# Cross-attention, 32 blocks on one core: the energy of a tile kept in one pair of PSUM banks

## The chip, the cores and the metric

The kernel runs on one core of a Trainium2 chip. Its time is the device time of one execution, in microseconds; lower is better. The median of three runs of the kernel before is 2110.47 us (2110.41 to 2111.45). One execution was profiled.

## The reference

For each of 32 blocks b there is an x and a y of 256 channels by 1024 columns, with weights shared by all blocks. In the reference's words, cut to the computation:

```python
x_q = einsum('oc,bcn->bno', w_qk, y)
x_k = einsum('oc,bcn->bon', w_qk, x)
x_v = einsum('oc,bcn->bon', w_v, x) + b_v
energy = einsum('bnc,bcm->bnm', x_q, x_k)                 # 1024 x 1024 a block
attention = softmax(energy, axis=-1)
attention = attention / (1e-07 + attention.sum(axis=1, keepdims=True))
x_r = einsum('bcn,bnm->bcm', x_v, attention)
x_r = relu(einsum('oc,bcn->bon', w_t, x - x_r) + b_t)
return x + x_r
```

All of it is float32. The kernel folds the weights: G = w_qk^T w_qk once, then energy = y^T (G x); and U = (w_t w_v) x plus a bias, so that the output needs one product U times attention and one w_t x.

## The kernel before, in words

**Stages of a block.** (1) *Energy*: eight tiles of 128 rows by 1024 columns (class `Energy`, L411 to L464). (2) *G x of the next block* (class `Keys`, `pg` in the profile), and *U of the next block* (class `Values`, `pu`). (3) *Column sums*: `columns` and `inverse` turn the sums over rows, kept in `acc`, into a row of reciprocals `rc`. (4) *Attention* (class `Attention`, `po`): VectorE multiplies the exponentials by both reciprocals (`normal`), forms sums of quarters (`mix`, tile `et`), and TensorE multiplies.

**Seven products.** G x, U and the attention product are each written as a product of 2x2 quarters with seven quarter products (class `Seven`, methods p1 to p7): products 1, 6, 7 and 4 add up in the accumulator `one`, 5 and 3 in `two`, 2 in `three`. Between them ScalarE keeps copies (`p1s`, `p5s`, `w`) because the next product is added onto the same bank; `p6` must wait for `p1s`, `p3` for `p5s`, and `p7` for `w`. VectorE's `c11`, `c12`, `c22` and ScalarE's `c21` combine them.

**The energy of a tile.** y and G x are each split into three forms (high, low and a mixture) in a reduced float32 type, and the energy comes from three products of equal forms. For each half of 512 columns, `products` issues 2 + 2 + 2 matmuls: forms 0 and 1 into one bank, form 2 into another. `gather` has ScalarE copy the first bank, scaled by -(1+2^-12), to SBUF (tile `es`), and VectorE add the second bank to it with one custom instruction that writes the sum to `e` in SBUF and leaves the running minimum of each row in `nm`. When both halves are there, `exp` (ScalarE) makes the exponentials in place in `e` with the row sum `rs`, and `share` (VectorE) takes the reciprocal `ri` of `rs` and adds `e` times `ri` into `acc`. The loop staggers them: with the products of tile n go `exp` of n-1 and `share` of n-2.

**PSUM.** There are eight banks of 512 float32 columns; `bank(name)` takes the next free one of a rotating pool of eight.

**Order.** `InOrder` (L62 to L76) chains every instruction of TensorE, VectorE, ScalarE and GpSimd behind the one written before it, so each of these engines works in the order of the program text, and almost every row of the profile has the line of this helper, L73; the tiles tell the rows apart. SyncE issues the loads and stores. GpSimd issues the accumulating DMAs (`accumulate`) that form sums and splits in memory, and does U's bias and sums in `factors`. The text around the change, at the end of the energy of a block that has a next one (L728 to L750), is: `g.p1`, `g.p5`, `exp` of tile 7, `share` of tile 6, `g.p2`, `g.c11`, `share` of tile 7, `g.p6`, `columns`, `g.p3`, `g.c12`, `g.p7`, `g.c22`, then `un.p1`, `un.p5`, `un.p2`, `un.p6` and `inverse`. The last block has no next one: there the end of the attention of the block before it (`before.xpart`, `before.epart`) follows the energy.

**Start.** Before the loop the kernel loads the weights, makes G, the transposed weights (`turned_weights`, bank `pt`), their product (`value_weights`, `pw`), and the bias of U (`value_bias`, `pb`, with `bvs` written by VectorE), with the first G x and U among them.

Of the kernel before, what the change touches and what calls it, by code (L numbers as in the profile page):

```python
# [9 lines left out]
F32 = mybir.dt.float32  # L10
F32R = mybir.dt.float32r
AF = mybir.ActivationFunctionType
ALU = mybir.AluOpType
AX = mybir.AxisListType
# [3 lines left out]
def kernel(  # L18
# [23 lines left out]
    B, C, N = x.shape  # L42
    P = 128
    KC = C // P
    NT = N // P
    MB = 512
    MH = N // MB
# [5 lines left out]
    BIG = 3.0e38  # L53
    UP = 4096.0
    UNDER = 1.0 - 2.0**-13
    OVER = 1.0 + 2.0**-12

    const = ctx.enter_context(tc.tile_pool(name="const", bufs=1))
    xp = ctx.enter_context(tc.tile_pool(name="xp", bufs=2))
    ps_m = ctx.enter_context(tc.tile_pool(name="ps_m", bufs=8, space=bass.MemoryType.PSUM))  # L60

    class InOrder:  # L62

# [13 lines left out]

    pe, dve, act, pool = (InOrder(g) for g in (nc.tensor, nc.vector, nc.scalar, nc.gpsimd))

    def bank(name):  # L80
        return ps_m.tile([P, MB], F32, tag="m", name=name)

    loaded = {}

    def load(b, pieces=1):
        to = xp.tile([P, KC, N], F32, tag="x", name=f"x_{b}")
        from_ = x[b].rearrange("(k p) n -> p k n", p=P)
        W = KC // pieces
        for j in range(pieces):
            nc.sync.dma_start(to[:, ts(j, W)], from_[:, ts(j, W)])  # L90
        loaded[b] = to
# [43 lines left out]
    behind = const.tile([P, 1], F32, name="behind")  # L135
    parts = const.tile([P, NB, NG + 1], F32, name="parts")
    dve.memset(parts[:, :, NG], EPS)
    idle = bank("idle")
    for _ in range(5):
        pe.matmul(idle[:, :P], few, few, start=True, stop=True)  # L140
    make_identity(nc, ident)
# [19 lines left out]
        return w, (a11, a12, s4, a22, s1, s2, s3)  # L161


    pg = [bank(f"pg_{i}") for i in range(KC)]
    for i in range(KC):
        for k in range(KC):
            pe.matmul(
# [1 line left out]
            )  # L169
    _, g_left = lefts("g", pg, UP)  # L170

    def turned_weights():

        pt = [bank(f"pt_{i}") for i in range(KC)]
        for i in range(KC):
            for k in range(KC):
                pe.transpose(pt[i][:, ts(k, P)], wt[:, k, ts(i, P)], ident)
        return lefts("wtT", pt)

    def value_weights(wtT):  # L180

        pw = [bank(f"pw_{i}") for i in range(KC)]
        for i in range(KC):
            for k in range(KC):
                pe.matmul(
                    pw[i][:, :C], wv[:, k, ts(i, P)], wtT[:, k, :], start=(k == 0), stop=(k == KC - 1)
                )
        return lefts("wvtT", pw, -1.0)[1]

    def value_bias(wtT):  # L190

        pb = bank("pb")
        for k in range(KC):
            dve.tensor_scalar(bvs[:, k], few, bv[:, k], None, ALU.add)
        for k in range(KC):
            pe.matmul(pb[:, :C], bvs[:, k], wtT[:, k, :], start=(k == 0), stop=(k == KC - 1))
        act.mul(bu.rearrange("p k c -> p (k c)"), pb[:, :C], -1.0)
        act.mul(nbt[:, :, 0], bt[:, :, 0], -1.0)
# [7 lines left out]
    def temp(tag, name):  # L206
        return cp.tile([P, MB], F32, tag=tag, name=name)
# [82 lines left out]
    class Seven:  # L290
# [3 lines left out]
        def __init__(self, name, b):  # L294
            self.name = name
            self.b = b

        def bank(self, j):
            return bank(f"p{self.name}{j}_{self.b}")

        def kept(self, p, tag):
            s = temp(tag, f"{self.name}{tag}_{self.b}")
# [107 lines left out]
    class Energy:  # L410
# [3 lines left out]
        def __init__(self, b, n, yf, gf):  # L414
            self.b, self.n = b, n
            self.yf, self.gf = yf, gf
            self.low = BIG

        def products(self, h):
            self.sums = [bank(f"pe{j}_{self.b}_{self.n}_{h}") for j in range(2)]  # L420
            for j in range(3):
                for k in range(KC):
                    pe.matmul(
                        self.sums[j // 2],
                        self.yf[:, j, k, ts(self.n, P)],
                        self.gf[:, j, k, ts(h, MB)],
                        start=(k == 0 and j != 1),
                        stop=(k == KC - 1 and j != 0),
                    )

        def gather(self, h):


            s = temp(("p1s", "p5s")[h], f"es_{self.b}_{self.n}_{h}")
            act.mul(s, self.sums[0], -OVER)
            nm = sp.tile([P, 1], F32, tag=f"nm{h}", name=f"nm_{self.b}_{self.n}_{h}")
            dve.tensor_tensor_reduce(
                out=e[:, self.n, ts(h, MB)],
                in0=self.sums[1],
                in1=s,  # L440
                scale=1.0,
                scalar=self.low,
                op0=ALU.add,
                op1=ALU.min,
                accum_out=nm,
            )
            self.low = nm

        def exp(self):
            self.rs = sp.tile([P, 1], F32, tag="rs", name=f"rs_{self.b}_{self.n}")  # L450
            row = e[:, self.n, :]
            act.activation(row, row, AF.Exp, bias=self.low, scale=-1.0, accum_out=self.rs)

        def share(self):

# [213 lines left out]
    g.split.high(0)  # L669
    g.split.high(1)  # L670
    u_left = value_weights(wtT)
    for i in range(KC):
        g.split.low(i)
    for i in range(KC):
# [9 lines left out]
    u.p6()  # L684
    u.p3()
    u.p7()
    value_bias(wtT)
    u.c11()
    u.c12()
    u.c22()  # L690
# [2 lines left out]
    for b in range(B):  # L693
        more = b + 1 < B
        rows = []

        for n in range(NT):
            now = Energy(b, n, q.to, g.split.to)
            rows.append(now)
            now.products(0)  # L700
            if n == 0:
                e = ep.tile([P, NT, N], F32, tag="e", name=f"e_{b}")
                acc = one.tile([P, N], F32, tag="acc", name=f"acc_{b}")
            now.gather(0)
            now.products(1)
            now.gather(1)
            if n == 0:
                if b == 0:
                    u.p4()
                    u.c21()  # L710
                    xsteps[1]()
                    xsteps[2]()
                elif more:
                    load(b + 1)
                if b == 0:
                    ur, usteps = u.factors()
                    for step in usteps:
                        step()
                if more and b > 0:
                    xn, xsteps = summed(b + 1)  # L720
            if n > 0:
                rows[n - 1].exp()
            if n > 1:
                rows[n - 2].share()
            if more and b > 0 and n in (2, 4, 6):
                xsteps[n // 2 - 1]()

        if more:  # L728
            q = Queries(b + 1)
            for i in range(KC):  # L730
                q.load(i, nc.sync.dma_start)
            g = Keys(b + 1, xn)
            g.p1()
            g.p5()
            rows[-1].exp()
            rows[-2].share()
            g.p2()
            g.c11()
            rows[-1].share()
            g.p6()  # L740
            columns(b)
            g.p3()
            g.c12()
            g.p7()
            g.c22()
            un = Values(b + 1, xn)
            un.p1()
            un.p5()
            un.p2()
            un.p6()  # L750
        else:
            before.xpart(before.one, 7, True)
            rows[-1].exp()
            rows[-2].share()
            before.epart(before.one, 7)
            ur, usteps = u.factors()
            now = Attention(b, xr, ur)
            now.begin()
            rows[-1].share()
            columns(b)  # L760
            for step in usteps:
                step()
            before.p7s = temp("w", "p7s")
            act.copy(before.p7s, before.one)
        rc = inverse(b)
        if more:
            q.parts(0)
            q.lower(0)
            un.p3()
            g.p4()  # L770
            g.c21()
            un.p7()
            q.parts(1)
            q.lower(1)
            q.mixed(0)
            g.split.parts(0)
            q.mixed(1)
            g.split.lower(0)

            def between():  # L780
                g.split.parts(1)
                g.split.lower(1)
                g.split.mixed(0)
                g.split.mixed(1)

            now = Attention(b, xr, ur)
            now.begin()
            now.run(un, between=between)
            pool.tensor_copy(behind, now.t4[:, HT - 1, :1])
            if b + 2 < B:  # L790
                now.close()
                ur, usteps = un.factors()
                for step in usteps:
                    step()
            else:
                now.epart(now.two, 3, (3,))
                now.c12()
                now.put()
            before = now
            xr, u = xn, un  # L800
        else:
            before.end()
            now.run(None, before)
            now.finish()
# [30 lines left out]
```

## Time and profile before

| | us |
|---|---|
| median of three runs | 2110.47 |
| profiled execution, its own time | 2108.64 |
| its span, first to last instruction | 2106.9 |
| TensorE busy (share of the span) | 2081.3 (99%) |
| VectorE busy | 1815.0 (86%) |
| ScalarE busy | 1171.9 (56%) |
| GpSimd busy | 673.3 (32%) |
| one block, energy start to energy start (1005.65 to 1070.68) | 65.03 |

The granted TensorE clock is at full speed in all of the span. Rows of the timeline give the start of an instruction (or of a run of like ones, with their count), what it took, and in brackets the idle time of the engine before it and what ended that. The start of the next instruction on the same engine is often earlier than the end of the one before, since the engines overlap the end of one with the start of the next; so costs in a queue are read from start to start. "po" is the attention product, "pe" the energy, "pg" G x, "pu" U.

### The profile page before, as it was taken

The page shows a single profiled execution, that of the slowest core. Times are in us where ns is not written, and L with a number is a line of the kernel's source. Part 1 is how long each engine was busy: PE and PEld are TensorE (multiplying, and loading weights), DVE is VectorE, ACT ScalarE, POOL GpSimd, SP SyncE. Part 2 cuts the span into 40 slices and gives each one's busy share as a digit, 9 for nine tenths or more (in the row PEclk, how much of TensorE's full clock was granted, in tenths as well). Part 3 has the DMA queues.
Part 4 walks back from the last instruction along what each step waited for, and adds up shares of the span by engine and source line. Part 5 has one row for each costly group of instructions (what it writes and reads, how often), then busy time and mean ns, then how long its engine had stood idle before and what let it go on. Part 6 is the DMA issues. An engine that isn't in the chain of part 4 may idle for free.

```text
span 2106.9 us, 23473 instructions
## 1 busy us (share of the span) xinstructions
PE 2081.3 (99%) x7586; PEld 1286.3 (61%) x7586; DVE 1815.0 (86%) x3032; ACT 1171.9 (56%) x1794; POOL 673.3 (32%) x574
## 2 busy tenths in 40 slices
PE   8999999999999999999999999999999999999998
PEld 6556665566665666556666556655566655666564
DVE  6898888998888988889888898888998888988898
ACT  5556554566455664556655556554566455664562
POOL 3322333323333133332333322333323333133321
PEclk9999999999999999999999999999999999999999
DMA  4665577665776656766557766577665676656740
GB/s 140 163 127 142 133 175 170 129 145 130 167 173 136 148 132 151 180 159 129 138 134 184 168 123 144 131 175 170 129 147 129 166 179 140 138 131 152 180 95 30
DMA packets 107802, 306.14 MB, mean 145 GB/s; under 512 B 10656, under 2 KB 11424, under 8 KB 107680
## 3 DMA queue, kind: packets, MB, share of 16 engines
q0 software_dynamic: 57040, 170.68, 44.2%
q1 hardware_dynamic: 50496, 133.85, 18.5%
q8 instruction: 60, 0.98, 0.2%
q14 instruction: 62, 0.51, 0.1%
q10 hardware_dynamic: 144, 0.13, 0.0%
HBM read 124.78 MB, written 33.55 MB: 75 GB/s over the span
## 4 chain that ended last, share of the span: by engine, by line
PE 62%; DVE 29%; issue 4%; ACT 1%; DMA 1%; DVEq 0%; POOL 0%; ACTq 0%; POOLq 0%
PE pe L73 31%; PE po L73 29%; DVE e L73 14%; DVE acc L73 4%; DVE et L73 4%; DVE gfr L73 3%; DVE rc L73 2%; DVE sc L73 1%; PE pu L73 1%; DVE parts L73 1%; ACT es L73 1%; DVE ri L73 0%; DMA gf<-gfr 0%; PE pg L73 0%; DMA gf<-gf 0%
## 5 line engine op out<-in xcount | busy, mean ns | idle before, releaser
L73 PE MATMUL pe<-gf,yf 128*128 128x512 f32 x3072 | 715.6, 393 | 0.9 <-DMA gf<-gf 0.9
L73 PEld LDWEIGHTS pe<-gf,yf 128*128 128x128 f32 x3072 | 576.6, 188 | 134.3 <-issue 16.2
L73 ACT ACTIVATE es<-pe 128x512 f32<-128x512 f32 x512 | 304.4, 595 | 172.2 <-PE pe L73 171.9
L73 PE MATMUL po<-et,us 128*128 128x512 f32 x768 | 353.9, 597 | 11.7 <-DVE et L73 11.7
L73 DVE SCALAR_TENSOR_TENSOR e<-e,ri,rc 128x512 f32<-128x512 f32 x512 | 347.4, 745 | 1.1
L73 DVE SCALAR_TENSOR_TENSOR acc<-e,ri,acc 128x1024 f32<-128x1024 f32 x224 | 288.6, 1288 | 8.0
L73 ACT ACTIVATE e<-e,nm 128x1024 f32<-128x1024 f32 x256 | 292.6, 1143 | 0.6 <-DVE nm L73 0.6
L73 PEld LDWEIGHTS po<-et,us 128*128 128x128 f32 x768 | 142.8, 190 | 207.3 <-issue 158.6
L73 DVE CUSTOM_DVE_ANT_0 e<-pe,es,nm 128x512 f32<-128x512 f32 x256 | 192.2, 751 | 76.6 <-ACT es L73 51.5
L73 PE MATMUL po<-e,ut 128*128 128x512 f32 x512 | 225.0, 592 | 1.0 <-DVE e L73 1.0
L73 POOL DMA_DIRECT2D yf<-yfr x62 | 53.1, 857 | 524.0 <-ACT yf L73 508.7
L73 DVE CUSTOM_DVE_ANT_0 e<-pe,es 128x512 f32<-128x512 f32 x256 | 175.5, 686 | 41.5 <-ACT es L73 41.2
L73 ACT ACTIVATE z<-po,bt 128x512 f32<-128x512 f32 x31 | 21.4, 690 | 334.2 <-DMA out_dram<-z 231.8
L73 PEld LDWEIGHTS po<-e,ut 128*128 128x128 f32 x512 | 97.2, 190 | 123.8 <-issue 107.4
L73 DVE TENSOR_TENSOR et<-e 128x1024 f32<-128x1024 f32 x128 | 153.6, 1220 | 4.4
L73 POOL TENSOR_TENSOR ut<-ut,bu 128x1024 f32<-128x1024 f32 x64 | 152.6, 2438 | 0.7 <-ACT ut L73 0.7
L73 POOL DMA_DIRECT2D gf<-gf x62 | 53.1, 856 | 295.5 <-DMA gf<-gfr 255.3
L73 DVE SCALAR_TENSOR_TENSOR z<-z,x 128x512 f32<-128x512 f32 x96 | 128.7, 1341 | 3.3
L73 PE MATMUL po<-e,us 128*128 128x512 f32 x256 | 125.4, 592 | 0.0
L73 ACT ACTIVATE yf<-yf 128x1024 fp32r<-128x1024 f32 x124 | 124.2, 1049 | 2.0
L73 ACT ACTIVATE gf<-gf 128x1024 fp32r<-128x1024 f32 x124 | 124.2, 1049 | 2.0
L73 POOL DMA_DIRECT2D xs<-xs x31 | 37.2, 1201 | 254.6 <-DMA xs<-in_x_dram 245.2
(110 smaller groups left out, 2749.1 us busy)
## 6 DMA issues: line engine op xcount, KB each, us to landing
yfr<-in_ctx_dram SPq DMA_DIRECT2D x64, 512.0 KB, 5.7
out_dram<-z SPq DMA_DIRECT2D x128, 256.0 KB, 3.5
x<-in_x_dram SPq DMA_DIRECT2D x31, 1024.0 KB, 7.5
xs<-in_x_dram SPq DMA_DIRECT2D x62, 512.0 KB, 5.0
yf<-yfr POOLq DMA_DIRECT2D x62, 512.0 KB, 5.1
yf<-yf POOLq DMA_DIRECT2D x62, 512.0 KB, 7.9
gf<-gfr POOLq DMA_DIRECT2D x62, 512.0 KB, 10.3
gf<-gf POOLq DMA_DIRECT2D x62, 512.0 KB, 5.2
```

The costliest lines, as they stand in the source:

```text
L73: self.last = getattr(self.engine, name)(*args, **kwargs)
```

## The change

All eight banks become one tile `banks`, and every user is given its place. A tile's energy has a pair of adjacent banks, one for each half, by its number: pairs 0 to 3 in turn (in the last block pairs 0 to 2). G x sits in banks 0, 1, 2 (those of tiles 4 and 5), U in 3, 4, 5, and the attention product in 6, 7, 1.

Forms 0 and 1 of both halves go to the pair (`first`), ScalarE scales the pair in place in PSUM with one instruction of 1024 columns, and form 2 is then added by TensorE onto the scaled numbers (`second`). VectorE only takes the minimum of 1024 columns from PSUM, and `exp` reads PSUM and writes `e`. Tile 7 is scaled in halves. The loop is staggered by one more: with `first` of tile n go `second` of n-1, `exp` of n-2 and `share` of n-3. At the start, `bvs` is written and `value_bias` done early; U's `p4`, `c21` and `factors` of the first block move from after tile 0 to after tile 1.

```diff
-    ps_m = ctx.enter_context(tc.tile_pool(name="ps_m", bufs=8, space=bass.MemoryType.PSUM))
+    ps_m = ctx.enter_context(tc.tile_pool(name="ps_m", bufs=1, space=bass.MemoryType.PSUM))
+    banks = ps_m.tile([P, 8, MB], F32, name="banks")
-    def bank(name):
-        return ps_m.tile([P, MB], F32, tag="m", name=name)
+    def bank(j):
+        return banks[:, j]
...
     _, g_left = lefts("g", pg, UP)
+    for k in range(KC):
+        dve.tensor_scalar(bvs[:, k], few, bv[:, k], None, ALU.add)
...
     def value_bias(wtT):
-        pb = bank("pb")
-        for k in range(KC):
-            dve.tensor_scalar(bvs[:, k], few, bv[:, k], None, ALU.add)
+        pb = bank(6)
...
+            last = name == "o" and b == B - 1
+            first = name == "u" and b == 0
+            self.places = {
+                "g": (0, 1, 2),
+                "u": (6, 4, 5) if first else (3, 4, 5),
+                "o": (7, 4, 5) if last else (6, 7, 1),
+            }[name]
         def bank(self, j):
-            return bank(f"p{self.name}{j}_{self.b}")
+            return bank(self.places[(1, 5, 2).index(j)])
...
-            self.low = BIG
-        def products(self, h):
-            self.sums = [bank(f"pe{j}_{self.b}_{self.n}_{h}") for j in range(2)]
...
-        def gather(self, h):
...
+            at = 2 * (n % (4 if b + 1 < B else 3))
+            self.pair = banks[:, at : at + 2]
+        def products(self, forms, halves=range(MH)):
+            for h in halves:
+                for j in forms:
+                    for k in range(KC):
+                        pe.matmul(
+                            self.pair[:, h],
+                            self.yf[:, j, k, ts(self.n, P)],
+                            self.gf[:, j, k, ts(h, MB)],
+                            start=(j == 0 and k == 0),
+                            stop=(j == 2 and k == KC - 1),
+                            skip_group_check=True,
+                        )
+        def first(self):
+            if self.n + 1 < NT:
+                self.products((0, 1))
+                act.mul(self.pair, self.pair, -OVER)
+                return
+            for h in range(MH):
+                self.products((0, 1), (h,))
+                act.mul(self.pair[:, h], self.pair[:, h], -OVER)
+        def second(self):
+            self.products((2,))
+            self.low = sp.tile([P, 1], F32, tag="nm", name=f"nm_{self.b}_{self.n}")
+            dve.tensor_reduce(self.low, self.pair.rearrange("p h m -> p (h m)"), AX.X, ALU.min)
         def exp(self):
-            row = e[:, self.n, :]
-            act.activation(row, row, AF.Exp, bias=self.low, scale=-1.0, accum_out=self.rs)
+            act.activation(
+                e[:, self.n, :],
+                self.pair.rearrange("p h m -> p (h m)"),
+                AF.Exp,
+                bias=self.low,
+                scale=-1.0,
+                accum_out=self.rs,
+            )
...
     u_left = value_weights(wtT)
+    value_bias(wtT)
...
     u.p7()
-    value_bias(wtT)
...
             now = Energy(b, n, q.to, g.split.to)
             rows.append(now)
-            now.products(0)
+            now.first()
...
-            now.gather(0)
-            now.products(1)
-            now.gather(1)
-            if n == 0:
-                if b == 0:
-                    u.p4()
-                    u.c21()
-                    xsteps[1]()
-                    xsteps[2]()
-                elif more:
-                    load(b + 1)
-                if b == 0:
-                    ur, usteps = u.factors()
-                    for step in usteps:
-                        step()
-                if more and b > 0:
-                    xn, xsteps = summed(b + 1)
             if n > 0:
-                rows[n - 1].exp()
+                rows[n - 1].second()
+            if b == 0 and n == 1:
+                u.p4()
+                u.c21()
+                xsteps[1]()
+                xsteps[2]()
+                ur, usteps = u.factors()
+                for step in usteps:
+                    step()
+            if more and b > 0 and n == 0:
+                load(b + 1)
+                xn, xsteps = summed(b + 1)
             if n > 1:
-                rows[n - 2].share()
+                rows[n - 2].exp()
+            if n > 2:
+                rows[n - 3].share()
...
             g = Keys(b + 1, xn)
+            rows[-1].second()
+            rows[-2].exp()
+            rows[-3].share()
             g.p1()
-            g.p5()
             rows[-1].exp()
             rows[-2].share()
+            g.p5()
             g.p2()
             g.c11()
             rows[-1].share()
...
         else:
+            rows[-1].second()
+            rows[-2].exp()
+            rows[-3].share()
             before.xpart(before.one, 7, True)
             rows[-1].exp()
             rows[-2].share()
```

More of the change, by code (lines that the diff above doesn't have):

```diff
@@ L137 @@
     dve.memset(parts[:, :, NG], EPS)
-    idle = bank("idle")
+    idle = bank(7)
     for _ in range(5):
@@ L161, in lefts @@
         return w, (a11, a12, s4, a22, s1, s2, s3)
-    pg = [bank(f"pg_{i}") for i in range(KC)]
+    pg = [bank(3 + i) for i in range(KC)]
     for i in range(KC):
@@ L170 @@
     _, g_left = lefts("g", pg, UP)
+    for k in range(KC):
+        dve.tensor_scalar(bvs[:, k], few, bv[:, k], None, ALU.add)
     def turned_weights():
-        pt = [bank(f"pt_{i}") for i in range(KC)]
+        pt = [bank(6 + i) for i in range(KC)]
         for i in range(KC):
@@ L180, in value_weights @@
     def value_weights(wtT):
-        pw = [bank(f"pw_{i}") for i in range(KC)]
+        pw = [bank(4 + i) for i in range(KC)]
         for i in range(KC):
@@ L416, in __init__ @@
             self.yf, self.gf = yf, gf
-            self.low = BIG
-        def products(self, h):
-            self.sums = [bank(f"pe{j}_{self.b}_{self.n}_{h}") for j in range(2)]
[L421 to L429, printed above, removed]
@@ L431, in gather @@
-        def gather(self, h):
[L434 to L447, printed above, removed]
+            at = 2 * (n % (4 if b + 1 < B else 3))
```

## The prediction, made before the changed kernel ran

> **What bounds the kernel now.** I read the page first, then the timeline of one block from the middle (energy from 1006 us) engine by engine, then the start and the last block.
>
> ```profile
> PE 2081.3 (99%) x7586; PEld 1286.3 (61%) x7586; DVE 1815.0 (86%) x3032; ACT 1171.9 (56%) x1794; POOL 673.3 (32%) x574
> ...
> PE 62%; DVE 29%; issue 4%; ACT 1%; DMA 1%; DVEq 0%; POOL 0%; ACTq 0%; POOLq 0%
> ```
>
> TensorE is almost never idle, yet the chain that ended last runs through VectorE for 29%. Both are true because, in each block, a stretch of VectorE work ends just late enough to hold TensorE for a moment. TensorE's timeline:
>
> ```profile
> 1002.62 3.60 PE L73 MATMUL po<-et,ut 128*128 128x512 f32 x8
> 1005.65 22.36 PE L73 MATMUL pe<-gf,yf 128*128 128x512 f32 x96
> 1027.85 1.02 PE L73 MATMUL pg<-x,g 128*128 128x512 f32 x2
> ...
> 1032.14 1.11 PE L73 MATMUL pg<-xs,gs 128*128 128x512 f32 x2
> 1033.08 1.05 PE L73 MATMUL pu<-wvtT,x 128*128 128x128 f32 x8
> ...
> 1048.74 1.88 PE L73 MATMUL po<-et,us 128*128 128x512 f32 x4
> 1050.95 1.98 PE L73 MATMUL po<-et,us 128*128 128x512 f32 x4 [0.33 <-DVE et L73]
> 1052.78 1.02 PE L73 MATMUL po<-xs,wtTs 128*128 128x512 f32 x2
> ```
>
> A pair of float32 matmuls takes 0.86 us from start to start, so one takes 0.429. The eight po from 1002.62 end their slots at 1006.05, and the 96 energy matmuls fill 1006.05 to 1027.85: 0.227 each, 2.72 us a tile, no idle time. p7 of G x (1032.14) needs 0.94 instead of 0.86: 0.08 lost to the copy `w`. The four et matmuls from 1048.74 should end at 1050.45; the next begin at 1050.95 and take 1.83 instead of 1.72: 0.61 lost, waiting for `et`. VectorE, from the last energy matmul to that wait:
>
> ```profile
> 1029.16 0.75 DVE L73 CUSTOM_DVE_ANT_0 e<-pe,es,nm 128x512 f32<-128x512 f32 x1 [0.17 <-DVE nm L73]
> ...
> 1031.23 0.16 DVE L73 RECIPROCAL ri<-rs 128x1 f32<-128x1 f32 x1
> 1031.42 1.28 DVE L73 SCALAR_TENSOR_TENSOR acc<-e,ri,acc 128x1024 f32<-128x1024 f32 x1
> 1032.62 0.68 DVE L73 TENSOR_TENSOR gfr<-pg,gp1s 128x512 f32<-128x512 f32 x1
> 1033.22 0.15 DVE L73 RECIPROCAL ri<-rs 128x1 f32<-128x1 f32 x1
> 1033.41 1.28 DVE L73 SCALAR_TENSOR_TENSOR acc<-e,ri,acc 128x1024 f32<-128x1024 f32 x1
> 1034.73 1.25 DVE L73 TRANSPOSE_TENSOR_REDUCE parts<-acc 128x32 f32<-128x1024 f32 x1
> ...
> 1049.68 1.22 DVE L73 TENSOR_TENSOR et<-e 128x1024 f32<-128x1024 f32 x1
> ```
>
> `columns` begins 6.88 us after the energy's last matmul slot (1034.73 less 1027.85). From there VectorE runs gapless to the `et` that TensorE waits for at 1050.95. So a block lasts as long as this tail of VectorE says: energy end to `columns`, plus a fixed 16.2 us, plus TensorE's rest.
>
> **The energy stage.** Matmuls keep their number and shapes: nothing. VectorE per tile before: two custom instructions and their read-outs, 1.54 us from start to start (1019.48 to 1021.02). After: one minimum of 1024 columns. No row has it; nearest is the 512-column TENSOR_TENSOR from PSUM, 0.68 us long and 0.60 to the next start, and the 1024-column one in SBUF, 1.22 and 1.14. I take 1.14 (1.22 until its result is there). Bounds: 0.76 (the 1024-column `acc<-e,ri`, 764 ns) and 1.37 (two customs of 686). With `share` at 1.39 (1031.23 to 1032.62) VectorE needs 2.53 of the 2.72 a tile instead of 2.93: it no longer lags, but waits for TensorE.
>
> Here the rows and a rule part. The Trainium skill (VectorE: DVE Perf Modes, Rules for kernel authors) calls `tensor_reduce` the slowest VectorE operation on a hot path and advises against it; going by the rule alone, swapping a custom operation for it would cost VectorE time, while by the rows above the stage gets 0.40 us a tile cheaper. No row before shows the reduction itself.
>
> ScalarE per tile before: 0.50 + 0.50 + 1.13. After: the in-place scaling, bounded by two copies (1.00) and by half-length rows (0.60 for 512, 1.05 for 1024: 0.50 + 0.45 = 0.95), and `exp` at 1.13 (1028.15 to 1029.28, from SBUF; a copy of 512 out of PSUM takes 0.59 and the one row out of SBUF 0.72, so I add nothing for PSUM): 2.08 of 2.72. `second` of a tile starts a whole tile period after its `first`, so the scaling has 2.7 us for 1.2: hidden; without that cover it would cost 1.2 a tile. Pairs come free 1.3 us before reuse.
>
> The Trainium skill (ScalarE: Activation LUTs, "What happens when an exp ACTIVATE runs") says that ScalarE writes PSUM faster than SBUF; no row before has such a write. By it the scaling would only get shorter, and the sum stays as it is, for it hides in any case.
>
> **The tail, where it counts.** The stagger is one tile deeper and VectorE now waits for tile 6's `second`, with `share` of tile 4 queued behind. Time from the end of that slot, Z; the energy ends at Z+0.91 (four matmuls). A result is seen 0.26 after its slot (up1s at 1034.23, slot end 1033.97). Queue: minimum 6 at 0.26, share 4 at 1.40, minimum 7 at 2.79, share 5 at 3.93, share 6 at 5.32, `c11` at 6.71 (0.60), share 7 at 7.31, `columns` 1.51 later (1033.22 to 1034.73) at 8.82. That is 7.91 after the energy, against 6.88: the block is 1.03 us longer by VectorE's tail.
>
> **TensorE meets a new wait as well.** `p3` needs `p5s`, which ScalarE now does after `exp` of tile 7, which needs minimum 7: its result at 4.01, `exp` at 4.05, `p5s` at 5.18 to 5.77, and a matmul 0.15 later (in p7's case `gw` ended at 1032.07 and the slot slid to 1032.22): 5.92. TensorE arrives after `second` 7, p1, p5, p2, p6: 0.91 + 4 x 0.857 = 4.34. Wait: 1.58. It absorbs p7's 0.08 and up to 0.61 of the `et` wait, so by this path a block is 0.89 longer. The longer path counts, not the sum: 1.03, with 1.58 at p3 and some 0.14 left at `et`. `p6` finds `p1s` at 3.3, before 3.48. G x's banks are read out by `exp` 4 and 5 before Z+1. ScalarE's splits and the DMAs behind them (yf, gf) follow U's copies and so shift with TensorE; SP's loads and POOL's sums keep their places. Behind p3 wait `c12`, U and all of TensorE. 31 blocks: 31 x 1.03 = 31.9.
>
> **Last block.** With three pairs, `first` of tile n+3 waits for `exp` of n. Cycle: 0.15 + 1.82 (eight matmuls) + 0.26 + 0.95 + 1.14 = 4.32 against 2.72, for tiles 3 to 7: 5 x 1.60 = 8.0. Its energy before took 22.99 (2038.19 to 2061.18), 1.20 over 96 slots, mostly a wait of 0.94 for gf's mixed form, which `second` needs later: -1.2. The tail: 7.31 (no c11) against 7.04, plus up to 0.82 if the last sum again meets POOL (2.10 instead of 1.28): +0.7. Together +7.5.
>
> **Start.** The first energy began at slot 29.42 (28.56 and four matmuls of `pb`), after `pb` had waited 2.74 for `bvs`, VectorE's last job:
>
> ```profile
> 20.14 1.16 PE L73 MATMUL pu<-wvtT,x 128*128 128x128 f32 x8 [1.12 <-ACT wvtT L73]
> ...
> 28.56 1.10 PE L73 MATMUL pb<-wtT,scratch 128*128 128x256 f32 x4 [2.74 <-DVE scratch L73]
> 29.31 3.10 PE L73 MATMUL pe<-gf,yf 128*128 128x512 f32 x12
> ```
>
> Now `bvs` (0.47) lies in VectorE's 1.49 idle before 10.06 (b_v lands at 2.6 + 5.6 = 8.2; a later landing would push c11), and `pb` lies in the 1.12 wait at 20.14. But `pb` and `pu` share bank 6: U's p1 waits for `bu` on ScalarE, 20.85 instead of 20.14. Energy at 24.71 + 0.89 + 0.7 = 26.3: -3.1. The moved p4 costs the same 0.89; its c21 and factors end 2.7 us later on POOL, 42 becoming 45, with first use after 66: hidden (2.7 if not). The two accumulating DMAs moved with them stay ahead of the factors on POOL's queue and land before block 1's G x at 50 (the copy-sum was issued at 24.6, the last at 29.95).
>
> **Sum.** 31.9 + 7.5 - 3.1 = 36.3. The profiled execution took 2108.64, so 2144.9; the median of the runs lies 1.83 above it: 2146.8. I say 2147.
>
> **Rivals.** (a) *The minimum is quick*, 0.76 a tile. Both paths shorten by 0.76 a block, to +0.27: 8.4 + 6.7 - 3.1, 2122. For: the scaled copy's 764 ns. Against: every PSUM reader in the rows goes at one column a cycle (686, 751, 680 for 512).
> (b) *ScalarE becomes the bound*, if the in-place scaling takes 1.9, a read and a write pass. Then 1.9 + 1.13 = 3.03 a tile, 0.31 over TensorE, 8 x 32 x 0.31 = 79: about 2226. Decides from 1.59. Against: the copies from PSUM at 0.60.
> (c) *Not slower: the energy matmuls go faster.* They are spaced 0.227 while half a float32 slot is 0.2145. If what holds them is the change of bank between forms (the bank was changed after four and two; now after four), 3072 x 0.0125 = 38 us come back and the time is 2108, no change. It decides from 0.2165 (less than 0.2% slower), and is nil at 0.2152, faster below. Against: the spacing is the same within forms and between them.
>
> **Numbers.** Forecast 0.80, (a) 0.06, (b) 0.04, (c) 0.10, in which I count any way of not being slower that I don't see. A difference under 0.2% (4 us) can't be told from none. Slower takes the forecast, (a) and (b): 0.90; (c) is split, 0.05 to faster and 0.05 to same. The range takes the minimum's bounds: 0.76 gives 2122, 1.37 gives 2 x 0.23 x 31 = 14 more, 2161; two more for the last block's tail: 2122 to 2163.
>
> **What would show it.** Right: a block period of 66.1; PE idle about 1.6 before the sixth G x product, named after `p5s`; `columns` 7.9 after the last energy matmul slot; a reduction row near 1.2 us; PE idle for `e` (exp) at tiles 3 to 7 of the last block alone; the first energy at 26.3. Wrong: a reduction row under 1.0 or over 1.3, idle TensorE inside the energy of other blocks, a matmul spacing off 0.227, or no wait at p3.

## The result, and the profile after

The changed kernel's median is 2149.99 us (2146.82 to 2150.2, five runs) against 2111.45 (2110.41 to 2112.2, five runs): the ratio is 1.018, 95% interval 1.0165 to 1.0195, so the change makes the kernel 1.8% slower. The profiled execution took 2146.82 with a span of 2144.9, 38.0 longer than the span before. Three stretches, cut at the first row of each energy in TensorE's timeline, add up to it:

| stretch | before | after | difference | predicted |
|---|---|---|---|---|
| start, to the first energy of block 0 | 29.31 | 26.30 | -3.0 | -3.1 |
| 31 blocks, to the first energy of the last block | 2008.49 | 2040.34 | +31.85 | +31.9 |
| last block, to the end of the span | 69.10 | 78.26 | +9.2 | +7.5 |

The page of the kernel after, its engines, its chain of waits and two groups:

```profile
PE 2085.0 (97%) x7586; PEld 1286.2 (60%) x7586; DVE 1778.6 (83%) x2264; ACT 1145.6 (53%) x1570; POOL 674.7 (31%) x574
...
PE 88%; DVE 7%; ACT 3%; issue 1%; DMA 0%; SPq 0%; DVEq 0%; ACTq 0%
...
L73 DVE TENSOR_REDUCE nm<-banks 128x1 f32<-128x1024 f32 x256 | 313.2, 1223 | 195.2 <-PE banks L73 184.0
L73 ACT ACTIVATE banks<-banks 128x1024 f32<-128x1024 f32 (+1 forms) x288 | 263.4, 915 | 190.2 <-PE banks L73 188.5
```

VectorE and ScalarE both have less to do (VectorE 36 us less), and the kernel is slower. The reduction takes 1.223 us, where I had put 1.22, and VectorE now waits 184 us for TensorE ahead of it: it no longer lags inside the energy. What counts is the end of the energy. TensorE's timeline of a block from the middle (all PSUM tiles are now called `banks`; their inputs tell the products apart):

```profile
1018.49 22.37 PE L73 MATMUL banks<-gf,yf 128*128 128x512 f32 x96
1040.70 1.02 PE L73 MATMUL banks<-x,g 128*128 128x512 f32 x2
1041.56 1.02 PE L73 MATMUL banks<-xs,gs 128*128 128x512 f32 x2
1042.41 1.02 PE L73 MATMUL banks<-x,g 128*128 128x512 f32 x2
1043.27 1.02 PE L73 MATMUL banks<-xs,gs 128*128 128x512 f32 x2
1045.58 1.13 PE L73 MATMUL banks<-x,gs 128*128 128x512 f32 x2 [1.28 <-ACT gp5s L73]
1046.54 1.02 PE L73 MATMUL banks<-xs,gs 128*128 128x512 f32 x2
...
1063.06 3.76 PE L73 MATMUL banks<-et,us 128*128 128x512 f32 x8
1066.66 1.02 PE L73 MATMUL banks<-xs,wtTs 128*128 128x512 f32 x2
...
1084.57 0.80 PE L73 MATMUL banks<-gf,yf 128*128 128x512 f32 x1
```

The energy takes what it took (22.37 against 22.36). The fifth G x product, p3 (the prediction's list of signs calls it the sixth, a slip: its sum counts four products ahead of it), should begin at 1044.13 and begins at 1045.58; with 0.10 more in its own slots TensorE loses 1.55 there, and the releaser is `gp5s`, as forecast. The wait for `et` has shrunk from 0.61 to 0.17 (eight matmuls in 3.60 instead of 3.43). The block lasts 66.08, where 66.06 was worked out. VectorE and ScalarE at the same place:

```profile
1040.06 1.23 DVE L73 TENSOR_REDUCE nm<-banks 128x1 f32<-128x1024 f32 x1
1041.20 0.15 DVE L73 RECIPROCAL ri<-rs 128x1 f32<-128x1 f32 x1
1041.39 1.28 DVE L73 SCALAR_TENSOR_TENSOR acc<-e,ri,acc 128x1024 f32<-128x1024 f32 x1
1042.60 1.22 DVE L73 TENSOR_REDUCE nm<-banks 128x1 f32<-128x1024 f32 x1
...
1048.62 1.25 DVE L73 TRANSPOSE_TENSOR_REDUCE parts<-acc 128x32 f32<-128x1024 f32 x1
```

```profile
1043.85 1.11 ACT L73 ACTIVATE e<-banks,nm 128x1024 f32<-128x1024 f32 x1 [0.84 <-DVE nm L73]
1044.86 0.19 ACT L73 ACTIVATION_READ_ACCUMULATOR e<-banks,nm 128x1 f32 x1
1044.95 0.58 ACT L73 COPY gp5s<-banks 128x512 f32<-128x512 f32 x1
```

The reader sees both paths here. On VectorE: minimum 6, share 4, minimum 7, and so on to `columns` at 1048.62, which is 7.92 after the energy (7.91 worked out, 6.88 before). On ScalarE: minimum 7 ends at 1043.82, exp 7 follows, then p5s, then TensorE's p3.

### The profile page after: what moved, and what is told of

Same layout as the page of the kernel before. It is cut to its first block, busy times and chain, and to the rows that moved or that the text cites. A ratio compares the mean times of both kernels' runs of the same rounds, so it can differ in the third digit from the quotient of the medians.

```text
span 2144.9 us, 21782 instructions
## 1 busy us (share of the span) xinstructions
PE 2085.0 (97%) x7586; PEld 1286.2 (60%) x7586; DVE 1778.6 (83%) x2264; ACT 1145.6 (53%) x1570; POOL 674.7 (31%) x574
## 4 chain that ended last, share of the span: by engine, by line
PE 88%; DVE 7%; ACT 3%; issue 1%; DMA 0%; SPq 0%; DVEq 0%; ACTq 0%
PE banks L73 88%; DVE nm L73 4%; DVE acc L73 2%; ACT e L73 2%; ACT gp5s L73 1%; DVE e L73 0%; DMA yfr<-in_ctx_dram 0%; ACT banks L73 0%; DVE et L73 0%; DVE ri L73 0%; ACT gf L73 0%; DVE parts L73 0%; DVE z L73 0%; DVE gfr L73 0%; DVE rc L73 0%
## 5 line engine op out<-in xcount | busy, mean ns | idle before, releaser
L73 PE MATMUL banks<-gf,yf 128*128 128x512 f32 x3072 | 716.9, 394 | 6.7 <-ACT e L73 6.7
L73 PEld LDWEIGHTS banks<-gf,yf 128*128 128x128 f32 x3072 | 576.3, 188 | 141.7 <-issue 14.8
L73 DVE TENSOR_REDUCE nm<-banks 128x1 f32<-128x1024 f32 x256 | 313.2, 1223 | 195.2 <-PE banks L73 184.0
L73 ACT ACTIVATE banks<-banks 128x1024 f32<-128x1024 f32 (+1 forms) x288 | 263.4, 915 | 190.2 <-PE banks L73 188.5
L73 PE MATMUL banks<-et,us 128*128 128x512 f32 x768 | 350.7, 597 | 0.8 <-DVE et L73 0.8
L73 ACT ACTIVATE e<-banks,nm 128x1024 f32<-128x1024 f32 x256 | 284.7, 1112 | 45.1 <-DVE nm L73 45.1
L73 PEld LDWEIGHTS banks<-et,us 128*128 128x128 f32 x768 | 143.2, 190 | 192.8 <-issue 161.7
L73 PE MATMUL banks<-e,ut 128*128 128x512 f32 x512 | 225.0, 592 | 3.1 <-DVE e L73 3.1
L73 PE MATMUL banks<-e,us 128*128 128x512 f32 x256 | 125.3, 592 | 0.0
L73 PE MATMUL banks<-et,ut 128*128 128x512 f32 x256 | 115.1, 592 | 0.0
```

The costliest lines, as they stand in the source:

```text
L73: self.last = getattr(self.engine, name)(*args, **kwargs)
```

## The experiments

**Two paths, taken away one by one.** The prediction says that a block is as long as the longer of two paths that both begin with the minimum of tile 6: VectorE's tail up to `columns` and on to `et`, and TensorE's wait at p3 for ScalarE's copy. If so, shortening one alone gives little, and shortening both gives much. Rivals say that one of them is the cost and the other only goes with it.

*One: the copy first.* This takes p3's wait away and leaves VectorE alone.

```diff
             g.p1()
+            g.p5()
             rows[-1].exp()
             rows[-2].share()
-            g.p5()
             g.p2()
```

> ScalarE's copy p5s is written before the exp of tile 7 again; nothing else differs from the changed kernel. Theory (a block is as long as the longer of two paths, TensorE's wait at p3 and VectorE's tail up to the columns): the wait of 1.56 at p3 goes, but the copy w now stands behind exp 7 (w 5.15 to 5.73 after the end of tile 6's second), so p7 loses about 0.7; VectorE's tail stays at 7.9 after the energy, so the saved time comes back as a wait for et, and the block stays at 66.06: 2150, within 4 us. Rival (the p3 wait is what the change costs): 1.56 - 0.7 = 0.9 less a block, 27 less: about 2122.

Measured: 2149.39 (2146.39 to 2150.49), ratio to before 1.0174 (1.0159 to 1.0189): no different from the changed kernel. TensorE's timeline of this run:

```profile
1043.34 1.02 PE L73 MATMUL banks<-x,gs 128*128 128x512 f32 x2
1044.79 1.13 PE L73 MATMUL banks<-xs,gs 128*128 128x512 f32 x2 [0.42 <-ACT gw L73]
...
1061.60 1.92 PE L73 MATMUL banks<-et,us 128*128 128x512 f32 x4
1064.06 1.98 PE L73 MATMUL banks<-et,us 128*128 128x512 f32 x4 [0.54 <-DVE et L73]
```

p3 begins on time, p7 loses 0.69 to `w`, and the rest comes back further on: 0.20 before p4 (where `c22` on VectorE ends just ahead of it) and 0.85 at `et`. That is 1.74 in all, against 1.55 and 0.17 in the changed kernel, and the block stays at 66.07. The wait named in the profile of the changed kernel, 1.55 us in each of 31 blocks and the largest idle time on its busiest engine, was worth nothing by itself.

*Two: the sum early.* This shortens VectorE's tail by one share and leaves ScalarE's order. The share that is taken out behind `rows[-2].exp()` is taken out in the last block's branch too.

```diff
             if n > 1:
                 rows[n - 2].exp()
-            if n > 2:
-                rows[n - 3].share()
+                rows[n - 2].share()
...
             rows[-1].second()
             rows[-2].exp()
-            rows[-3].share()
```

> VectorE's share of a tile is staggered by two tiles, as exp is, not by three, so one share (1.39) less lies behind the energy; TensorE and ScalarE keep their order. Theory (longer of two paths): VectorE's tail falls from 7.9 to 6.5 after the energy, but the wait at p3 stays (one share is still ahead of tile 7's minimum), so the block only falls from 1.03 to 0.89 over before: 0.14 x 31 = 4, and 1 to 2 in the last block: 2144. Rival (VectorE's tail alone is the cost, the p3 wait only takes the place of the et wait): 1.39 less a block, 43 less: 2107.

Measured: 2138.25 (2137.0 to 2138.88), ratio 1.0123 (1.0108 to 1.0138). `columns` is 6.46 after the energy, and p3 still waits:

```profile
1041.77 1.02 PE L73 MATMUL banks<-xs,gs 128*128 128x512 f32 x2
1044.00 1.13 PE L73 MATMUL banks<-x,gs 128*128 128x512 f32 x2 [1.21 <-ACT gp5s L73]
```

The block falls to 65.83, 0.25 less than changed and not the 0.14 expected: TensorE loses 1.48 at p3, 0.07 less than in the changed kernel (minimum 6 begins 0.71 before the energy's end instead of 0.64), and the last 0.17 at `et` is gone. The last block gives 3.0 instead of 1 to 2. Of the 43 us of the rival 12 appear.

*Both.* The two diffs together.

> Both edits, the copy p5s before exp 7 and the share staggered by two. Theory: with both paths shorter the gain appears that neither gives alone: p7 still loses 0.7 to w, the et wait (0.61 before) is gone, the block is 65.0: 33 less in 31 blocks and 1 to 2 in the last: 2116. If the two edits simply added (each path a cost by itself): 2122 and 2107 would add to 2079.

Measured: 2111.19 (2109.18 to 2112.94, ten runs), ratio 0.9998 (0.9988 to 1.0008). Alone the edits gave 0.6 and 11.7 us against the changed kernel, together 38.8. The block is 64.97 (65.0 expected); the time is 5 us under the 2116 that were expected, of which, by the profiled executions, the 31 blocks give 1.7 (34.7 less for 33) and the last block about 1 (2.8 less for 1 to 2). That neither path is much of a cost by itself, and that the longer one sets the block, is shown by these three runs.

*And tile 7's minimum ahead of a share.* With both edits p7 still waits for `w`, behind an exp that waits for VectorE. Here tile 5's `share` leaves the loop's last turn for the place behind tile 7's `second`, in both branches. The cut is against the run with both edits.

```diff
                 rows[n - 2].exp()
-                rows[n - 2].share()
+                if n + 1 < NT:
+                    rows[n - 2].share()
...
             rows[-1].second()
             rows[-2].exp()
+            rows[-3].share()
```

> As with both edits, and the minimum of tile 7 on VectorE ahead of the share of tile 5. Theory: exp 7 follows p5s at once (3.6 after the end of tile 6's second), w is ready at 5.3, p7 loses about 0.2, VectorE's tail stays at 6.5: block 64.6, 45 less than the changed kernel in 31 blocks: 2103, faster than before. Rival (ScalarE's queue at the tail, not VectorE's order, is the limit): no change from the run with both edits, 2116.

Measured: 2099.2 (2098.08 to 2101.53), ratio 0.994 (0.9925 to 0.9955): faster than before (2103 expected).

```profile
1021.29 1.02 PE L73 MATMUL banks<-x,gs 128*128 128x512 f32 x2
1022.28 1.13 PE L73 MATMUL banks<-xs,gs 128*128 128x512 f32 x2
```

The block is 64.60, p7 loses 0.23, and at `et` 0.03 is left: in the 31 blocks TensorE has next to nothing more to wait for. The order of VectorE's queue, and not ScalarE's, was what still cost.

**The last block and the start.** The edits of the run before, with the exp of a tile put ahead of the scaling two tiles on, in the last block alone, so that with three pairs the pair is free in time; and `pb` in bank 7.

```diff
-        pb = bank(6)
+        pb = bank(7)
...
+            early = not more and 1 < n < NT - 1
+            if early:
+                rows[n - 2].exp()
             now.first()
...
-                rows[n - 2].exp()
+                if not early:
+                    rows[n - 2].exp()
```

> The changed kernel with five edits: p5s before exp 7, share staggered by two, tile 7's minimum ahead of a share, the exp of two tiles back ahead of the scaling in the last block alone, and pb in bank 7. Theory: 64.6 a block; in the last block first of tile n+3 finds its pair free (exp ends 2.77 after the reduction's tile began, against 2.72), so its five waits of 1.66 go, about 8; U's p1 at the start no longer waits for bu, 0.7: 2094, 0.8% faster than before. Rival (the last block is bound by VectorE, whose rows there wait for POOL): the last block keeps its 30.5 us of energy and the time is 2102.

Measured: 2092.02 (2091.72 to 2093.53), ratio 0.9914 (0.99 to 0.9927), the fastest version here: 0.9% under before. TensorE's last block in the kernel before, in the changed kernel, and then in this one:

```profile
2037.80 1.71 PE L73 MATMUL pe<-gf,yf 128*128 128x512 f32 x5
2040.45 20.89 PE L73 MATMUL pe<-gf,yf 128*128 128x512 f32 x91 [0.94 <-DMA gf<-gf]
2061.18 1.02 PE L73 MATMUL po<-xs,wtTs 128*128 128x512 f32 x2
```

```profile
2066.64 7.86 PE L73 MATMUL banks<-gf,yf 128*128 128x512 f32 x32
2075.80 0.50 PE L73 MATMUL banks<-gf,yf 128*128 128x512 f32 x1 [1.30 <-ACT e L73]
...
2080.19 3.02 PE L73 MATMUL banks<-gf,yf 128*128 128x512 f32 x12 [1.35 <-ACT e L73]
2084.57 3.04 PE L73 MATMUL banks<-gf,yf 128*128 128x512 f32 x12 [1.36 <-ACT e L73]
...
2097.12 1.02 PE L73 MATMUL banks<-xs,wtTs 128*128 128x512 f32 x2
```

```profile
2022.46 4.46 PE L73 MATMUL banks<-gf,yf 128*128 128x512 f32 x17
2027.51 18.81 PE L73 MATMUL banks<-gf,yf 128*128 128x512 f32 x79 [0.59 <-DMA gf<-gf]
2046.15 1.02 PE L73 MATMUL banks<-xs,wtTs 128*128 128x512 f32 x2
```

With three pairs the tiles follow each other at 4.38 instead of 2.72, each waiting for an exp; with the exp earlier the five waits are gone and the energy takes 23.7 instead of 30.5. The wait for gf's mixed form, absent in the changed kernel, is back with 0.59; the run before this one had it too, with 0.47. With `pb` in bank 7 U's p1 no longer waits for `bu`: it begins at 22.77, and `bu` at 22.97. What that gives in time can't be read, for the start of this execution ran at a lower clock (below).

*The start alone.* Kernel before, with `bvs` and `value_bias` early and the pool of banks as it was.

```diff
     _, g_left = lefts("g", pg, UP)
+    for k in range(KC):
+        dve.tensor_scalar(bvs[:, k], few, bv[:, k], None, ALU.add)
...
         pb = bank("pb")
-        for k in range(KC):
-            dve.tensor_scalar(bvs[:, k], few, bv[:, k], None, ALU.add)
...
     u_left = value_weights(wtT)
+    value_bias(wtT)
...
     u.p7()
-    value_bias(wtT)
```

> The kernel before, with only bvs written and value_bias done early, banks still from the pool. Theory: the bias' matmuls fill the wait of 1.12 ahead of U's p1, the first energy begins at 24.71 + 0.89 = 25.6 where it began at 29.3: 3.7 less, 0.17%: 2107.7. Rival (something later in block 0 takes it back, the loads of block 1 or GpSimd's sums): 2111, no change.

Measured: 2107.67 (2107.2 to 2111.33, eleven runs), ratio 0.9988 (0.9979 to 0.9997): 3.2 us less by the medians. The one part of the change that gains does so by itself, as expected (3.7), though the interval, 0.6 to 4.4 us less, is wider than the gain. The start can't be read from its trace: the profiled execution, at 2109.91, had a lower clock there (below).

**The cover of the scaling.** I cost the in-place scaling at nothing, since ScalarE has time for it. Here half of it is done twice on tiles 0 to 5.

```diff
                 act.mul(self.pair, self.pair, -OVER)
+                if self.n < 6:
+                    act.mul(self.pair[:, 0], self.pair[:, 0], 1.0)
                 return
```

> The changed kernel with one more ScalarE instruction a tile, on tiles 0 to 5: half of the pair (512 columns) is multiplied by 1 in place, 0.5 more a tile, 48 x 31 + 48 times in all less tiles 6 and 7. Theory (ScalarE has 0.6 to spare in a tile's 2.72 and the scaling has a tile's time before form 2 is added): nothing inside the energy, the block stays at 66.06, 2150. Last block: its cycle contains the extra instruction, 5 x 0.5 = 2.5 more. Rival (ScalarE's in-place scaling is part of the cost): 6 x 0.5 = 3 more a block, 93 more: 2243.

Measured: 2160.21 (2158.36 to 2162.76), ratio 1.0236 (1.0222 to 1.025), 10 us over the changed kernel: nearer to the theory than to the rival's 93, but not nothing. The profiled execution is the longest of the four, 15.9 over that of the changed kernel. In it the block is 66.24, 0.16 to 0.18 longer. TensorE loses it at the first two matmuls of tile 0's `second`, on the half that was multiplied again (0.27 and 0.34 from start to start instead of 0.227): tile 0 has no `second` of an earlier tile between its `first` and its own, so its cover is 1.82 and not 2.72. Elsewhere in these blocks the extra 0.5 is hidden. The last block took 7.8 more, not 2.5. TensorE's rows there, and windows of it (busy time of each engine, clock in the third column from the right):

```profile
2085.15 3.04 PE L73 MATMUL banks<-gf,yf 128*128 128x512 f32 x12 [1.92 <-ACT e L73]
2090.16 4.58 PE L73 MATMUL banks<-gf,yf 128*128 128x512 f32 x12 [1.97 <-ACT e L73]
2096.70 4.60 PE L73 MATMUL banks<-gf,yf 128*128 128x512 f32 x12 [1.97 <-ACT e L73]
2103.16 4.61 PE L73 MATMUL banks<-gf,yf 128*128 128x512 f32 x12 [1.86 <-ACT e L73]
2108.71 3.92 PE L73 MATMUL banks<-gf,yf 128*128 128x512 f32 x16 [0.93 <-ACT e L73]
```

```profile
2075.00:2085.00 10.00, 7.91 (x33) 5.74 (x31) 6.79 (x6) 5.78 (x8) 5.33 (x3) 1.00 0.46 111
2085.00:2092.00 7.00, 4.88 (x16) 3.66 (x17) 2.05 (x3) 2.80 (x6) 0.00 (x0) 0.87 0.00 0
2092.00:2100.00 8.00, 6.04 (x17) 4.50 (x16) 2.58 (x3) 2.70 (x4) 0.00 (x0) 0.71 0.00 0
2100.00:2110.00 10.00, 7.21 (x23) 5.10 (x22) 4.66 (x6) 4.83 (x8) 0.00 (x0) 0.81 0.00 0
```

The granted clock fell to 0.71 to 0.87 for 25 us, with waits of 1.9 in every 5 to 6.5 us. The first cycle, before the twelve matmuls grew from 3.04 to 4.6, took 5.01, which is 0.63 over the 4.38 of the changed kernel. The next three took 6.54, 6.46 and 5.55. The first two of these hold an extra instruction and the third does not, so against 5.01, 5.01 and 4.38 they are 4.2 longer. An estimate from these rows is then 4.2 for the lower clock and 2.5 for the extra instructions of tiles 2 to 5 (4 x 0.63); some 1.1 is spread over the first three tiles, where 0.33 is a wait for gf's mixed form, and the tail.

## Why the prediction was right

The forecast of 2147 stood 3 us under the median, inside its range, and against the profiled execution, for which the sum was made, it was 2144.9 to 2146.82. The step from that execution to the median, which I took over from the kernel before as 1.83, was 3.2 here; so of the 3 us, 1.9 are of the sum and 1.3 of this step.

- *The tail of VectorE* was the largest term, 1.03 a block. `columns` came at 7.92 for 7.91, the block at 66.08 for 66.06. The reduction's length, for which no row stood, was taken from the nearest row and held: 1.223 for 1.22, 1.14 to the next start. The bounds of 0.76 and 1.37 were far wider than needed.
- *The wait at p3* came at 1.55 for 1.58, with 0.17 left at `et` for 0.14. That the two are not added was the step that decided the size. Added to the old waits, 1.58 would have given 49 us; alone, with the rest gone, 0.89 a block or 28. The runs with one path shortened show that both stand at nearly the same length, so neither could be seen as the cost from its own idle time.
- *The energy stage* cost nothing, as said: spacing 0.227 before and after, the scaling at 0.92 from start to start for 0.95. Rival (c), a faster spacing, and rival (b), a slow write to PSUM, both fell on these rows; rival (a) fell on the reduction's row. The premise of (c) was a misreading too: TensorE changes the bank four times a tile in both kernels, after 4, 2, 4 and 2 matmuls before and after 4, 4, 2 and 2 now. One statement was too broad: the scaling's cover is 2.7 for tiles 1 to 6, but 1.8 for tile 0, and tile 7's two halves have only four matmuls (0.91) between its `first` and its `second`. No row shows TensorE waiting there in these 31 blocks.
- *The last block* was the term that was mis-sized: +9.2 for +7.5. The cycle itself was right (4.38 for 4.32), and the energy 7.1 longer for 6.8. The rest is the tail after it: `columns` came 9.18 after the energy against 7.04 before, 2.1 more where I had 0.7. That 0.7 took 7.31 for the tail and about half of the 0.82 that one sum beside GpSimd's work would add. Two sums lay there, at 2.34 and 2.10 us instead of 1.28. VectorE's rows before, and after:

```profile
2066.09 2.10 DVE L73 SCALAR_TENSOR_TENSOR acc<-e,ri,acc 128x1024 f32<-128x1024 f32 x1
```

```profile
2101.73 2.34 DVE L73 SCALAR_TENSOR_TENSOR acc<-e,ri,acc 128x1024 f32<-128x1024 f32 x1
...
2104.17 2.10 DVE L73 SCALAR_TENSOR_TENSOR acc<-e,ri,acc 128x1024 f32<-128x1024 f32 x1
2106.30 1.25 DVE L73 TRANSPOSE_TENSOR_REDUCE parts<-acc 128x32 f32<-128x1024 f32 x1
```

U's sums on GpSimd start 4.6 after the energy in both kernels (2065.78 and 2101.72); VectorE had one sum left to do by then, and now has two. That GpSimd's work is what lengthens them is read from the rows lying side by side; no run took it away.

- *The start* came at 3.0 for 3.1, with less room than I gave it. The two additions for `bvs`, which I put at 0.47 inside 1.49 idle, lasted from 8.56 to 10.05, the second one 1.3 us instead of 0.28, beside GpSimd's sums, and `c11` began at 10.14, on time. In the run with the start alone they also waited 0.48 for b_v to land, and `c11` began at 10.19, 0.98 after p2's last slot where the changed kernel has 0.28; VectorE then had 2.57 of idle time, so nothing behind it shifted.

Against the rule weighed in the prediction (the Trainium skill, VectorE: DVE Perf Modes, Rules for kernel authors), the reduction was no slow operation here: 1.14 from start to start against 1.54 for the two custom instructions that it replaced, and VectorE's busy time fell by 36 us. The time was lost in the order, not in the operation. The other page's statement (the Trainium skill, ScalarE: Activation LUTs, Step-by-step: what each stage is for), that ScalarE writes PSUM faster than SBUF, is not settled by these rows. For 1024 columns, 1.01 in place in PSUM and 1.05 from SBUF to SBUF differ in where they read as well, and exp, which writes SBUF in both kernels, took 1.11 reading PSUM and 1.14 reading SBUF. For 512 columns out of PSUM, a scaling took 0.589 on average into PSUM and 0.595 into SBUF, and copies into SBUF took 0.57 to 0.60.

## What to carry to other kernels

A deeper stagger let VectorE keep up inside the energy, where TensorE had not waited for it, and made the end longer: when a stage ends, every step that was put off is still to be done, and the work after the stage waits for it. So cost a pipeline's change at its end, in order of each queue, and not by the busy time that it saves. And where two engines' paths end at nearly the same point, work out both and take the longer: idle time named in a profile can be worth nothing until the path beside it is shortened too.

## What the runs showed of the hardware

In five of the nine profiled executions the granted clock of TensorE is halved for a while at the start. Windows of the run with the start alone, 16 to 24 us, and then of the changed kernel (the clock is the third column from the right):

```profile
16.00:20.00 4.00, 3.01 (x5) 1.82 (x6) 1.98 (x3) 0.92 (x2) 1.35 (x1) 0.50 0.76 253
20.00:24.00 4.00, 4.00 (x16) 3.30 (x16) 1.06 (x5) 2.66 (x6) 0.00 (x0) 0.66 0.95 195
```

```profile
16.00:20.00 4.00, 3.63 (x14) 2.58 (x14) 1.36 (x2) 2.49 (x4) 1.35 (x1) 1.00 0.86 299
20.00:24.00 4.00, 3.19 (x29) 3.13 (x29) 3.39 (x7) 2.08 (x6) 0.00 (x0) 1.00 0.90 158
```

At 0.50 and 0.66 these eight microseconds hold 3.4 us less of matmul clock. What goes before is TensorE's wait for ScalarE's `gw` at about 13 us, then one of 1.9 for `gfr`, the same in all. In the nine profiled executions the first wait was 0.52, 1.13, 1.14 and 1.23 where the clock stayed at 1.00, and 1.51, 1.74, 1.81, 2.16 and 2.50 where it was halved. The waits of 1.86 to 1.97 in the last block of the run with more work on ScalarE went with a clock of 0.71 to 0.87, and the shorter ones of the changed kernel's last block (1.30 to 1.36) with 1.00. So waits of no more than 2.5 us, close together, go with a lower clock here; no run varied them alone, and what sets the bound is open. It bears on the comparison, for an edit that lengthens a short wait may cost clock as well.
